# Two-layer graph and expert kernel: the first layer's second expert product in seven block products, its shares computed at the listing

## The chip, the cores and the metric

One core of one Trainium2 chip. The metric is the device time of one execution in microseconds, the median of several runs. Matrices are float32. Engines: PE (TensorE, matmuls), DVE (VectorE), ACT (ScalarE), POOL (GpSimd), SP (SyncE, which issues most loads).

## The reference

Two layers over 3327 nodes with 256 features, each an aggregation over a sparse matrix followed by a mixture of 8 experts of which each node uses 2. Cut to layer 0 (layer 1 has another aggregation, Gelu and experts with 256 hidden units):

```python
x = x + relu(adj @ (layernorm(x) @ W) + b)
t = layernorm(x)
gate_scores = einsum('bsd,ed->bse', t, Wg) + bg
topk_scores, topk_idx = top_k(gate_scores, 2)
topk_probs = softmax(topk_scores)
combine = sum(topk_probs[..., None] * one_hot(topk_idx, 8), -2)
for e in range(8):
    h = relu(einsum('bsd,hd->bsh', t, W1[e]) + b1[e])   # 1024 hidden
    y = einsum('bsh,dh->bsd', h, W2[e]) + b2[e]
    out = out + combine[..., e:e+1] * y
x = x + out
```

## The kernel before, in words

Nodes are padded to 3328 = 26 tiles of 128. `adj` comes in 13 panels of 256 rows, each in two pieces of 128 x 3328, in a ring of six places.

**Aggregation of layer 0** (`aggregate_first`). Panels 0 and 1 run side by side, panels 2 to 11 as five pairs with seven block products in place of eight (`pair`, sums of pieces on DVE), panel 12 alone (`rest`, whose matmuls are on L495). A finished panel waits; `finish` (called in `rest` after slice `first + BEHIND`, 5) or the next pair first lists what was routed before (`listed`), then multiplies the waiting sums by W (`weigh`, L506), and then routes them (`route0`). ACT meanwhile counts signs of `adj` (`count`, L1369, eight activations per piece, each with a read of its accumulator), which layer 1 needs.

**Routing.** `scores` multiplies each tile by each row of the gating matrix `gate` on DVE (L659), `weights` ranks the eight scores (`rt_both` marks the two best, L697) and computes the shares: the difference `rt_d` of the two scores on DVE (L724), its Exp on ACT (L725), and 1/(1+e) and its rest on DVE (L727 to L729). `list_tokens` later counts places by matmuls of `rt_both` (L760, L761), copies shares (L755) and ids into the rows on POOL, and scatters the rows to the experts' lists `xlist` (L779).

**Experts of layer 0** (`experts`, H = 1024). The lists are cut into 30 blocks: 26 pairs of 256 rows and 4 singles of 128, the first 8 pairs early, the rest by a table that `plan` computes on DVE from the counts. A block's rows, its expert's W1, b1, W2 and b2 (2.6 MB) take two places of the ring, so three blocks are in flight; SP issues block t+3 when block t has left its places. `step(t)` calls in this order:

- `first`: for each of 8 groups of 128 hidden units two matmuls (L1171) into `ps_h`, evacuated by ACT with Relu and b1 (L1178) into `hT`;
- `turned` for block t+1: four transposes (L1157) into `ptb`, which shares the two PSUM buffers of `ps_h`, copied by DVE (L1161, `copy`);
- `second`: for each half of 128 rows, eight matmuls of 256 columns (L1209) into `ps_y`, then b2 added (L1216) and the row's share multiplied (L1217) on DVE, and the rows scattered by POOL to `ys` (L779).

[...]The order is settled at build: mostly that of the calls, but a call may be put ahead of one that would have to wait, unless `behind` or `issue_after` hold it. `step(0)` has `finish_last` between its two products: the listing of panels 10 and 11, then the weighing and routing of panel 12. The listing of panel 12 follows `step(1)`. Around the last blocks DVE adds outputs that are complete (`add_begun`, behind block 27) and takes their statistics (behind block 28), for layer 1.

**After it**: `load_gate(gates[1])` loads the gating matrix of layer 1 over that of layer 0, by POOL's queue, as soon as panel 12 is listed. `between` normalizes and projects for layer 1, whose aggregation starts at 769 us.

Of the kernel before, what the change touches and what calls it, by code (L numbers as in the profile page):

```python
# [10 lines left out]
F32 = mybir.dt.float32  # L11
BF16 = mybir.dt.bfloat16
I32 = mybir.dt.int32
AF = mybir.ActivationFunctionType
ALU = mybir.AluOpType
# [7 lines left out]
P = 128  # L23
NT = 26
NP = NT * P
D = 256
DC = D // P
# [3 lines left out]
NPAN = NP // PW  # L31
NCHUNK = 2
CJ = NT // NCHUNK
# [41 lines left out]
    return order + [q for q in range(LATE_PAIRS, LATE) if q not in order]  # L75


BEHIND = 5
BEGUN, FIRST_TILES, MORE_TILES = 12, 14, 22
WARM = 54  # L80
TIERS = 3
# [46 lines left out]
def gnn_moe_two_layers(  # L128
# [353 lines left out]
    def aggregate_first(b_sb, w, w_sb, begin, count, route, listed, freed):  # L482
# [69 lines left out]
            else:  # L552
                freed(pan, k)

        def rest(pan, first, hooks=()):
            hooks = dict(hooks)
            for j in range(first, NT):
                add(pan, j)
                if j == first + BEHIND:
                    finish()  # L560
                if j in hooks:
                    hooks[j]()
            g = sums_of()
            for c in range(DC):
                copy(g[:, c, :], sums[pan][c])
            waiting.append((pan, g))
# [76 lines left out]
        sums[NPAN - 1] = banks[0:2]  # L643
        for _ in range(NCHUNK):
            count_next()
        rest(NPAN - 1, 0, {CJ: layer0.turn_first})
        return finish

    def rows_of(a, t0, n):
# [64 lines left out]
        nc.vector.tensor_reduce(v, m, AX.X, ALU.add)  # L714
        return v

    def weights(sc, n, bias=None):


        if bias is not None:  # L720
            nc.vector.tensor_tensor(sc, sc, bias.unsqueeze(1).to_broadcast([P, n, E]), ALU.add)
        sel, top, both = top_two(sc, n)
        d = work.tile([P, n], F32, name="rt_d", bufs=2)
        nc.vector.tensor_tensor(d, top[:, :, 1], top[:, :, 0], ALU.subtract)  # L724
        nc.scalar.activation(d, d, AF.Exp)  # L725
        w = work.tile([P, n, K], F32, name="rt_w", bufs=2)
        nc.vector.tensor_scalar(w[:, :, 0], d, 1.0, None, ALU.add)  # L727
        nc.vector.reciprocal(w[:, :, 0], w[:, :, 0])
        nc.vector.tensor_tensor(w[:, :, 1], w[:, :, 0], d, ALU.mult)  # L729
        return sel, both, w  # L730

    def normalized(t, n, on_scalar=False):

# [15 lines left out]

    def list_tokens(xns, sel, both, w, t0, n, xlist, group):  # L750

        for i, xn in enumerate(xns):
            at = 2 * i
            nc.gpsimd.tensor_copy(xn[:, :, 1, 0:D], xn[:, :, 0, 0:D])
            nc.gpsimd.tensor_copy(xn[:, :, :, WT], w[:, at : at + 2, :])  # L755
            nc.gpsimd.tensor_copy(xn[:, :, :, ID], ids[:, t0 + at : t0 + at + 2, :])
        pr = pst.tile([P, n, E], F32, name="pr", tag="pt")
        for g in range(n):
            i = t0 + g
            nc.tensor.matmul(pr[:, g, :], lhsT=before, rhs=both[:, g, :], start=True, stop=False)  # L760
            nc.tensor.matmul(pr[:, g, :], lhsT=ones_sq, rhs=cum[:, i, :], start=False, stop=True)  # L761
            nc.vector.tensor_tensor(cum[:, i + 1, :], cum[:, i, :], both[:, g, :], ALU.add)
        row = work.tile([P, n, E], F32, name="rt_row", bufs=2)
        nc.vector.tensor_tensor(
            row, pr, starts.unsqueeze(1).to_broadcast([P, n, E]), ALU.add
        )
        idx = work.tile([P, n * K], I32, name="rt_idx", bufs=2)
        nc.vector.tensor_copy(idx, chosen(sel, row, n).rearrange("p n k -> p (n k)"))
        for g in range(n):
            for k in range(K):  # L770
                q = g * K + k
                row_ = xns[g // 2][:, g % 2, k, :]
                d = scatter(xlist, idx[:, q : q + 1], row_, "rows" + group)
                tc.declare_no_dep(d.ins, group="early" + group, reason="not rows of full blocks")
                rows_written.append(d)
# [270 lines left out]
        nc.vector.tensor_tensor(aside, spare_, aside, ALU.subtract)  # L1046
        return end

    def experts(xlist, ys, group, fixed, n_hidden, func, w1T, b1, w2T, b2, copy, order_of_places, kept=None):

# [42 lines left out]
        def col_of(t):  # L1095
            return t if t < EARLY else order[t - EARLY]

        def groups_of(t):
            return SG if t < EARLY or order[t - EARLY] < LATE_PAIRS else 1
# [61 lines left out]
            copy(xT, pt)  # L1161
            return xT

        def first(xT, w1, bb1, n):

            hT = blk("narrow" if kept else "wide", hc_n * SB)
            hT = hT.rearrange("p (c b) -> p c b", b=SB)[:, :, 0 : n * P]
            for hc in range(hc_n):
                ps = psh.tile([P, n * P], F32, name="ps_h", tag="ph")
                for c in range(DC):  # L1170
                    nc.tensor.matmul(  # L1171
                        ps,
                        lhsT=w1[:, c, ts(hc, P)],
                        rhs=xT[:, c, :],
                        start=(c == 0),
                        stop=(c == DC - 1),
                    )
                nc.scalar.activation(hT[:, hc, :], ps, func, bias=bb1[:, hc : hc + 1])  # L1178
            return hT

        def second(t, late, hT):
            _, xb, _, _, w2, bb2 = loaded[t]
            col, n = col_of(t), groups_of(t)
            index = work.tile([P, SG], I32, name="index", bufs=6)[:, 0:n]
            with behind(last_y):
                if t < EARLY:
                    nc.vector.tensor_copy(index, xb[:, :, ID])
                else:
                    _, own, aside = late[0:3]
                    index_f = index.bitcast(F32)  # L1190
                    nc.vector.tensor_tensor(index_f, xb[:, :, ID], own[:, col, 0:n], ALU.mult)
                    nc.vector.tensor_tensor(index, index_f, aside[:, col, 0:n], ALU.add)
            if t >= own_n:
                e = expert(t, late, [PE, DVE])
                w2 = all_w2[:, ds(e, 1), :, :].rearrange("p o c d -> p (o c) d")
                bb2 = all_b2[:, ds(e, 1), :].rearrange("p o d -> p (o d)")
            if not kept:
                y = blk("narrow", SG * D).rearrange("p (g d) -> p g d", d=D)
            else:
                if not several:  # L1200
                    wide = blk("wide", H // P * SB)
                    for at in range(0, H // P * SB, SG * D):
                        y = wide[:, at : at + SG * D]
                        several.append(y.rearrange("p (g d) -> p g d", d=D))
                y = several.pop(0)
            for g in range(n):
                ps = psy.tile([P, D], F32, name="ps_y", tag="py")
                for hc in range(hc_n):
                    last_product[:] = [nc.tensor.matmul(  # L1209
                        ps,  # L1210
                        lhsT=hT[:, hc, ts(g, P)],
                        rhs=w2[:, hc, :],
                        start=(hc == 0),
                        stop=(hc == hc_n - 1),
                    )]
                nc.vector.tensor_tensor(y[:, g, :], ps, bb2, ALU.add)  # L1216
                last_y[:] = [nc.vector.tensor_scalar(  # L1217
                    y[:, g, :], y[:, g, :], xb[:, g, WT : WT + 1], None, ALU.mult
                )]
                d = scatter(ys, index[:, g : g + 1], y[:, g, :], "outputs" + group)  # L1220
                tc.declare_no_dep(d.ins, group="read" + group, reason="not rows read by then")
                outputs.append(d)

        ready = {}

# [5 lines left out]
        def step(late, end=always, place=None, between=None):  # L1231

            t = len(started)
            started.append(t)
            while len(loaded) < min(t + RING // places, end):
                load(late)
            if t not in ready:
                ready[t] = turned(loaded[t][1], groups_of(t))
            _, _, w1, bb1, _, _ = loaded[t]
            hT = first(ready.pop(t), w1, bb1, groups_of(t))  # L1240
            if between:
                between()
            if t + 1 < min(len(loaded), end):
                ready[t + 1] = turned(loaded[t + 1][1], groups_of(t + 1), place)
            second(t, late, hT)

        def steps_to(late, stop):
            while len(started) < stop:
# [116 lines left out]
    def count(pan, k, copied):  # L1365
# [7 lines left out]

    layer0 = experts(
        xlist0, ys0, "0", FIXED[0], H, AF.Relu, f0_w1T, f0_b1, f0_w2T, f0_b2,
        nc.vector.tensor_copy, BLOCKS0,
    )

    def tiles_of(pans):
# [36 lines left out]
        list_waiting()  # L1416


    load_gate(gates[1])
    by_feature(None, g1_wp, proj_sb)  # L1420
    nc.gpsimd.dma_start(out=gnn_b_sb, in_=g1_bg[0:1, :].partition_broadcast(P))
    ng = NPAN * PW // GROUP
# [86 lines left out]

    def between():  # L1510

        normal.clear()
        second.clear()
        waiting = []
# [42 lines left out]
    def after1(layer1, pan):  # L1557
# [1 line left out]
        list_waiting()  # L1559
        xns = normalized(t, n)  # L1560
        sc = scores(xns, n) if pan < NPAN - 1 else scores_by_product(by_features(xns[0], n), n, f1_r_sb)
        routed.append((xns, *weights(sc, n), t, n, xlist1, "1"))
        x_t = x[:, t : t + n, :]
        nc.gpsimd.tensor_tensor(x_t, x_t, xns[0][:, :, 0, 0:D], ALU.add)
        if pan == EARLY_PANS[1]:
# [278 lines left out]
```

## Time and profile before

| | |
|---|---|
| median of 3 runs | 1220.21 us (1218.53 to 1228.95) |
| profiled execution | 1222.4 us, span 1220.7 us |
| layer 0's aggregation | up to 302.3 us |
| layer 0's experts | 302.3 to 717.8 us |
| PE busy | 1176.8 us |
| DVE busy | 755.1 us |
| ACT busy | 524.4 us |
| POOL busy | 288.2 us |

The page sums up one execution. A group line names the source line, engine, operation, what it writes and reads, the shape and count, then busy time and the mean duration of one, then idle time of the engine ahead of it. The slices divide the span in 40 parts of 30.5 us and show the busy share in tenths. A timeline line has start, length, engine, line, operation, shape and count of a run of equal instructions, and in brackets how long the engine had been idle before it and what ended that. Every float32 matmul call shows as two instructions.

### The profile page before, as it was taken

The page shows a single profiled execution, that of the slowest core. Times are in us where ns is not written, and L with a number is a line of the kernel's source. Part 1 is how long each engine was busy: PE and PEld are TensorE (multiplying, and loading weights), DVE is VectorE, ACT ScalarE, POOL GpSimd, SP SyncE. Part 2 cuts the span into 40 slices and gives each one's busy share as a digit, 9 for nine tenths or more (in the row PEclk, how much of TensorE's full clock was granted, in tenths as well). Part 3 has the DMA queues.
Part 4 walks back from the last instruction along what each step waited for, and adds up shares of the span by engine and source line. Part 5 has one row for each costly group of instructions (what it writes and reads, how often), then busy time and mean ns, then how long its engine had stood idle before and what let it go on. Part 6 is the DMA issues. An engine that isn't in the chain of part 4 may idle for free. (4 is left out here: it accounts for less than half of the span.)

```text
span 1220.7 us, 18191 instructions
## 1 busy us (share of the span) xinstructions
PE 1176.8 (96%) x5689; PEld 1008.2 (83%) x5689; DVE 755.1 (62%) x2767; ACT 524.4 (43%) x977; POOL 288.2 (24%) x367
## 2 busy tenths in 40 slices
PE   8999999999899999999999999999999999988983
PEld 7888888888688888888888888888888888877863
DVE  7699999988761111111121359289999998784464
ACT  5689566521222222323222236985555542132331
POOL 1112233043421111111111110022242242264441
PEclk9999999999899999999999999999999999988996
DMA  9894747654376555756565946154455452556696
GB/s 344 187 317 189 246 160 202 226 178 139 99 243 209 185 191 172 263 177 219 195 213 181 366 160 230 56 186 180 143 196 186 149 185 66 175 176 213 207 294 214
DMA packets 123178, 241.59 MB, mean 198 GB/s; under 512 B 24480, under 2 KB 93120, under 8 KB 116160
## 3 DMA queue, kind: packets, MB, share of 16 engines
q1 hardware_dynamic: 108656, 205.59, 51.0%
q0 software_dynamic: 11136, 31.60, 7.0%
q10 hardware_dynamic: 3280, 3.15, 0.7%
q8 instruction: 47, 0.77, 0.3%
q14 instruction: 59, 0.48, 0.1%
HBM read 203.98 MB, written 36.33 MB: 197 GB/s over the span
## 5 line engine op out<-in xcount | busy, mean ns | idle before, releaser
L440 PE MATMUL ps_g<-s,ring 128*128 128x256 f32 x1352 | 294.2, 380 | 0.0
L440 PEld LDWEIGHTS ps_g<-s,ring 128*128 128x128 f32 x1352 | 256.3, 190 | 34.0
L1178 ACT ACTIVATE pad<-ps_h,ring 128x256 f32<-128x256 f32 (+1 forms) x282 | 128.3, 457 | 346.3 <-PE ps_h L1171 321.7
L1171 PE MATMUL ps_h<-pad,ring 128*128 128x256 f32 (+1 forms) x1184 | 259.0, 372 | 9.5 <-ACT pad L1178 6.0
L1171 PEld LDWEIGHTS ps_h<-pad,ring 128*128 128x128 f32 x1184 | 205.8, 193 | 55.0 <-ACT pad L1178 18.9
L1209 PE MATMUL ps_y<-ring,pad 128*128 128x256 f32 x928 | 209.7, 382 | 0.0
L659 DVE SCALAR_TENSOR_TENSOR rt_product<-xn,gate 128x256 f32<-128x256 f32 x400 | 195.1, 488 | 16.2 <-ACT xn L360 2.2
L779 POOL DMA_INDIRECT ys<-pad,index x114 | 112.9, 990 | 390.5 <-DVE pad L1217 259.4
L1209 PEld LDWEIGHTS ps_y<-ring,pad 128*128 128x128 f32 x928 | 173.9, 192 | 22.1 <-issue 0.2
L779 POOL DMA_INDIRECT xlist<-xn,rt_idx x104 | 114.5, 1101 | 154.4 <-DVE ln_nw L347 56.3
L1369 ACT ACTIVATE sign<-ring,below 128x416 bf16<-128x416 f32 x208 | 133.4, 642 | 11.6 <-DMA ring<-in_adjT 5.6
L470 PE MATMUL ps_g<-ring,pad 128*128 128x256 f32 x520 | 115.5, 380 | 0.7 <-DMA ring<-in_adjT 0.5
L1216 DVE TENSOR_TENSOR pad<-ps_y,ring 128x256 f32<-128x256 f32 x64 | 27.1, 423 | 136.2 <-PE ps_y L1209 127.8
L470 PEld LDWEIGHTS ps_g<-ring,pad 128*128 128x128 f32 x520 | 98.3, 190 | 14.8 <-DMA ring<-in_adjT 0.9
L1161 DVE COPY pad<-ptb 128x512 f32<-128x512 f32 (+1 forms) x29 | 18.9, 652 | 144.6 <-PE ptb L1157 143.6
L1534 ACT ACTIVATE ring<-ring 128x3328 f32<-128x3328 f32 x22 | 65.4, 2979 | 87.6 <-DVE ring L1533 50.2
L470 PE MATMUL ps_g<-ring,s 128*128 128x256 f32 x390 | 89.6, 379 | 0.1
L470 PEld LDWEIGHTS ps_g<-ring,s 128*128 128x128 f32 x390 | 74.1, 190 | 10.4 <-ACT xnT L538 0.5
L480 DVE TENSOR_TENSOR ring<-ring,ring 128x768 f32<-128x768 f32 (+1 forms) x80 | 79.8, 1013 | 0.0
L495 PE MATMUL ps_g<-ring,s 128*128 128x256 f32 x312 | 68.5, 380 | 3.0 <-ACT s L360 3.0
L495 PEld LDWEIGHTS ps_g<-ring,s 128*128 128x128 f32 x312 | 59.0, 190 | 11.6 <-ACT s L360 3.6
L1535 ACT ACTIVATE ring<-ring 128x3328 f32<-128x3328 f32 x22 | 65.4, 2977 | 0.6
(220 smaller groups left out, 1114.8 us busy)
## 6 DMA issues: line engine op xcount, KB each, us to landing
ring<-in_adjT SPq DMA_DIRECT2D x50, 1664.0 KB
ring<-in_f_w1T SPq DMA_DIRECT2D x30, 1024.0 KB
ring<-in_f_w2T SPq DMA_DIRECT2D x30, 1024.0 KB
ring<-xlist SPq DMA_DIRECT2D x52, 258.0 KB
ring<-in_f_w SPq DMA_DIRECT2D x36, 256.0 KB
ring<-ys SPq DMA_DIRECT2D x12, 512.0 KB
ring<-in_f_b SPq DMA_DIRECT2D x34, 128.0 KB
xlist<-h2T SPq DMA_DIRECT2D x16, 257.0 KB
```

The source lines that it names most:

```text
L440: nc.tensor.matmul(ps[it], lhsT=chunks[k][:, c, ts(it, P)], rhs=s[:, j, :], start=(j == 0), stop=(j == NT - 1),)
L470: nc.tensor.matmul(ps, lhsT=b[:, c, :], rhs=a[:, c, :], start=(first and c == 0), stop=(c == CJ - 1), skip_group_check=not first,)
L480: nc.vector.tensor_tensor(out[:, part, :], out[:, part, :], other[:, part, :], ALU.add)
L495: nc.tensor.matmul(sums[pan][c], lhsT=s[:, j, ts(c, P)], rhs=piece(pan, j // CJ)[:, j % CJ, :], start=(j == 0), stop=(j == NT - 1),)
L659: nc.vector.scalar_tensor_tensor(product, xn, 1.0, gate[:, e, :], ALU.mult, ALU.mult, accum_out=sc[:, g, e : e + 1],)
L779: d = nc.gpsimd.indirect_dma_start(out=a[:, :], out_offset=bass.IndirectOffsetOnAxis(ap=index, axis=0), in_=rows_, in_offset=None,)
L1171: nc.tensor.matmul(ps, lhsT=w1[:, c, ts(hc, P)], rhs=xT[:, c, :], start=(c == 0), stop=(c == DC - 1),)
L1178: nc.scalar.activation(hT[:, hc, :], ps, func, bias=bb1[:, hc : hc + 1])
L1209: last_product[:] = [nc.tensor.matmul(ps, lhsT=hT[:, hc, ts(g, P)], rhs=w2[:, hc, :], start=(hc == 0), stop=(hc == hc_n - 1),)]
L1369: nc.scalar.activation(sign, piece(pan, k)[:, :, ts(i, GROUP)], AF.Sign, bias=below, accum_out=positive[:, pan, i, k : k + 1],)
L1534: nc.scalar.activation(a, a, AF.Square)
L1535: nc.scalar.activation(a, a, AF.Tanh)
```

## The change

**Second product of layer 0, pairs from block 3 on.** With `hT` cut into A11, A12 (hidden halves, first 128 rows), A21, A22 (second 128 rows) and W2 into B11, B12, B21, B22 (hidden halves by feature halves), seven products of 128 rows, 512 hidden units and 128 columns take the place of eight. `prepare`, called ahead of `first`, makes four differences of W2 on DVE, which lie in `gate`, and scales b2 by each row's share into `y` on ACT. `difference` and the start of `second_seven` make four sums of `hT` on DVE, in tiles named xnT and h2T. Each finished product or sum of products is multiplied by the share and added to a quarter of `y` in one DVE instruction (eight per block). Two of the four PSUM tiles are used again while they hold a sum.

**Shares of layer 0.** `weights` leaves the difference; Exp, 1/(1+e) and the copy into the rows are called in `list_tokens`. Layer 1 keeps the old place (`now=True`).

**Others.** The listing in the last panel comes after slice 8 instead of 5. The turned rows of layer 0 are copied by ACT instead of DVE. `gate` is loaded for layer 1 at the start of `between`.

```diff
-BEHIND = 5
+BEHIND, LAST_BEHIND = 5, 8
...
-        rest(NPAN - 1, 0, {CJ: layer0.turn_first})
+        rest(NPAN - 1, 0, {CJ: layer0.turn_first}, LAST_BEHIND)
...
-        nc.scalar.activation(d, d, AF.Exp)
+        if now:
+            nc.scalar.activation(d, d, AF.Exp)
+            return sel, both, shares(d, n)
+        return sel, both, d
...
     def list_tokens(xns, sel, both, w, t0, n, xlist, group):
+        if group == "0":
+            nc.scalar.activation(w, w, AF.Exp)
         for i, xn in enumerate(xns):
             at = 2 * i
             nc.gpsimd.tensor_copy(xn[:, :, 1, 0:D], xn[:, :, 0, 0:D])
-            nc.gpsimd.tensor_copy(xn[:, :, :, WT], w[:, at : at + 2, :])
...
+        if group == "0":
+            w = shares(w, n)
+        for i, xn in enumerate(xns):
+            nc.gpsimd.tensor_copy(xn[:, :, :, WT], w[:, 2 * i : 2 * i + 2, :])
...
+        def prepare(t):
+            _, xb, _, _, w2, bb2 = loaded[t]
...
+            nc.vector.tensor_tensor(t1, halves(w2, 0, 1), halves(w2, 0, 0), ALU.subtract)
+            nc.vector.tensor_tensor(t2, b22, t1, ALU.subtract)
+            nc.vector.tensor_tensor(t4, b21, t2, ALU.subtract)
+            nc.vector.tensor_tensor(t3, b22, halves(w2, 0, 1), ALU.subtract)
+            y = blk("narrow", SG * D).rearrange("p (g d) -> p g d", d=D)
+            for g in range(SG):
+                nc.scalar.activation(y[:, g, :], bb2, AF.Copy, scale=xb[:, g, WT : WT + 1])
...
+        def difference(sums, hT):
+            a11, a21 = halves(hT, 0, 0), halves(hT, 0, 1)
+            nc.vector.tensor_tensor(sums[1][2], a11, a21, ALU.subtract)
...
                 nc.scalar.activation(hT[:, hc, :], ps, func, bias=bb1[:, hc : hc + 1])
+                if sums and hc == hc_n // 2 - 1:
+                    difference(sums, hT)
...
+        def second_seven(t, late, hT, sums):
...
+            nc.vector.tensor_tensor(s1, a21, a22, ALU.add)
+            nc.vector.tensor_tensor(s2, s1, a11, ALU.subtract)
+            nc.vector.tensor_tensor(s4, a12, s2, ALU.subtract)
+            ps_x, ps_q, ps_b, ps_z = (
+                psy.tile([P, P], F32, name="ps_y", tag="py") for _ in range(4)
+            )
+            def multiply(ps, a, b, first=True):
+                for c in range(hc_n // 2):
+                    last_product[:] = [nc.tensor.matmul(
+                        ps, lhsT=a[:, c, :], rhs=b[:, c, :], start=(first and c == 0),
+                        stop=(c == hc_n // 2 - 1), skip_group_check=not first,
+                    )]
+            def put_in(g, half_, ps):
+                part = y[:, g, ts(half_, P)]
+                last_y[:] = [nc.vector.scalar_tensor_tensor(
+                    part, ps, xb[:, g, WT : WT + 1], part, ALU.mult, ALU.add
+                )]
+            multiply(ps_x, a11, b11)
+            put_in(0, 0, ps_x)
+            multiply(ps_q, a22, t4)
+            put_in(1, 0, ps_q)
+            multiply(ps_b, a12, b21)
+            put_in(0, 0, ps_b)
+            multiply(ps_z, s1, t1)
+            put_in(1, 1, ps_z)
+            multiply(ps_x, s2, t2, False)
+            put_in(0, 1, ps_x)
+            multiply(ps_z, s4, b22, False)
+            put_in(0, 1, ps_z)
+            put(y, index, 0)
+            multiply(ps_x, s3, t3, False)
+            put_in(1, 0, ps_x)
+            put_in(1, 1, ps_x)
+            put(y, index, 1)
...
             _, _, w1, bb1, _, _ = loaded[t]
+            sums = prepare(t) if seven and t >= seven and groups_of(t) == SG else None
...
-        nc.vector.tensor_copy, BLOCKS0,
+        nc.scalar.copy, BLOCKS0, seven=3,
...
-    load_gate(gates[1])
...
     def between():
+        load_gate(gates[1])
```

## The prediction

> **What bounds the kernel now.** I read the page first: TensorE (PE) is busy 96% of the span and next to all of it in most slices, VectorE (DVE) is full only in the first quarter.
>
> ```profile
> PE 1176.8 (96%) x5689; PEld 1008.2 (83%) x5689; DVE 755.1 (62%) x2767; ACT 524.4 (43%) x977; POOL 288.2 (24%) x367
> ...
> PE   8999999999899999999999999999999999988983
> ...
> DVE  7699999988761111111121359289999998784464
> ```
>
> The change lies in the experts of layer 0, so next the timeline of PE there, 400 to 440 us: a block of 256 rows is first product, four transposes, second product, with no gap.
>
> ```profile
> 400.56 7.16 PE L1171 MATMUL ps_h<-pad,ring 128*128 128x256 f32 x32
> 407.55 0.60 PE L1157 MATMUL ptb<-ident,ring 128*128 128x128 f32 x4
> 407.98 7.07 PE L1209 MATMUL ps_y<-ring,pad 128*128 128x256 f32 x32
> 414.89 7.16 PE L1171 MATMUL ps_h<-pad,ring 128*128 128x256 f32 x32
> ```
>
> The starts give a block of 14.33 us: 6.99, 0.43 and 6.91. One matmul of the code is two instructions here (16 calls, x32), so an instruction of 256 columns takes 6.91 / 32 = 216 ns; the mean of 382 ns in the groups is a pipelined duration, not a price. From 400 to 690 us the windows view has PE busy 289.72 of 290 us, DVE 51.45 and ACT 79.89. So PE alone sets the time of this stage, and each ns taken from its stream counts.
>
> The new products have 128 columns. The group of that shape reads 24.8 us for 176 instructions, 141 ns each, but that takes in waits and pipeline ends. The timeline of PE at 554 us, in a single block (128 rows), is closer:
>
> ```profile
> 554.13 1.05 PE L1171 MATMUL ps_h<-pad,ring 128*128 128x128 f32 x8
> 555.02 0.60 PE L1209 MATMUL ps_y<-ring,pad 128*128 128x256 f32 x2
> 555.46 1.05 PE L1171 MATMUL ps_h<-pad,ring 128*128 128x128 f32 x8
> ```
>
> Eight take 555.02 - 554.13 = 0.89 us, 111.5 ns each, a new weight load in front of every one. (L1209 also stands here between matmuls that the code calls earlier: at build, a call may be put ahead of one that would wait.)
>
> Last the seam between aggregation and experts, 271 to 320 us, PE and then ACT:
>
> ```profile
> 271.92 5.34 PE L495 MATMUL ps_g<-ring,s 128*128 128x256 f32 x24
> 278.58 0.18 PE L760 MATMUL pr<-rt_both,before 128*128 128x8 bf16 x1 [1.32 <-DVE rt_both L697]
> ...
> 302.28 5.34 PE L1171 MATMUL ps_h<-pad,ring 128*128 128x256 f32 x24
> 311.63 3.78 PE L1171 MATMUL ps_h<-pad,ring 128*128 128x256 f32 x8 [4.01 <-ACT pad L1178]
> ...
> 315.46 2.94 PE L506 MATMUL ps_o<-proj_sb,xnT 128*128 128x256 f32 x8
> ```
>
> ```profile
> 305.93 0.47 ACT L1178 ACTIVATE pad<-ps_h,ring 128x256 f32<-128x256 f32 x1 [0.39 <-PE ps_h L1171]
> 311.01 0.21 ACT L725 ACTIVATE rt_d<-rt_d 128x4 f32<-128x4 f32 x1 [4.61 <-DVE rt_d L724]
> ```
>
> PE waits 1.32 us for the routing of a panel pair, then 4.01 us for ACT: in ACT's queue the Exp of L725 stands ahead of the evacuations of block 0, and it waits 4.61 us for DVE. After both waits PE runs slow: the windows view grants a clock of 0.78 from 277 to 284.6 us and 0.81 from 302.3 to 320.
>
> [...]
>
> **The change, part by part.**
>
> *Seven products.* Removed per pair: 16 calls, 32 instructions x 216 = 6.91 us. Added: 7 products x 4 calls x 2 = 56 instructions x 111.5 = 6.24 us. Gain 0.66 us. Of the 30 blocks of layer 0, 26 are pairs and 4 singles; from block 3 on, 23 pairs. 23 x 0.66 = **15.2 us**. The longest run of this shape in the trace is 8, so 56 in a row is bounded: 109 ns (the transposes, 0.43 us for 4) gives 18.5 us, 115 gives 10.8. I take 111.5.
>
> *DVE's new work.* Per block 8 sums and differences of 128x512 elements, at 0.69 us (L1293, 128x512, 689 ns[...]): 5.5 us. 8 evacuations of 128x128 from PSUM: the 128x256 one (L1216) takes 423 ns[...], between 200 and 423: 2.3 us. Index 0.3. Together 8.1 us (7.4 to 9.2) in a block of 13.67; 2.5 us of evacuation, copy and scaling go. Order: from the end of the first product, PE has transposes and three products, 0.43 + 3 x 0.89 = 3.1 us, until it needs s1. That is ready after the last ACT evacuation (0.65) and one sum, 1.4 us; s2 is ready at 2.1 and needed at 4.0, s4 at 2.8 and 4.9. The differences of w2 (2.8 us) run under the first product of the same block. So PE does not wait: cost 0. Without that cover the whole chain of 2.1 us would stand in front of the products.
>
> *ACT* gets the turned copy (0.59 us, L1161 on ACT) and two scalings of b2 (some 0.45 each) on top of 8 x 0.47: 5.3 us of 13.67. The copy has 6.2 us until the next block. The scalings stand ahead of block t's evacuations and need b2 of t and the scatter of block t-2 done, both over 10 us old. Cost 0. Loads: SP issues block t+3 when block t ends, as before; 2.6 MB take some 9 us of 13.67 (issued at 372.9, the DMA share falls at 382).
>
> *Exp at the listing.* The Exp is no longer ahead of block 0's evacuations: the 4.01 us wait goes. *Listing 3 slices later:* 3 x 4 x 216 = 2.6 us more work ahead of the listing's matmuls, more than 1.32: that wait goes, with the 1.8 us that the slow clock cost behind it (16 matmuls from 279.31 to 284.57, 5.26 us for 3.45). So the last panel ends at 302.28 - 3.1 = 299.2, block 0's first product at 306.1. Now the listing's matmuls need rt_both: DVE had it at 310.1, and sheds there the copy L1161 with the wait and slow scores around it, some 2.3 us: 307.8. The wait moves to PE itself, 1.7 us. Then the two panel products, 1.73 us: 309.8 where they ended at 318.23. Gain 8.4 us; if the wait costs a slow window again (8 x 0.21), 6.7. I take **7.5 us**. Behind the waiting matmuls stand the two products that feed DVE with the last panel; its routing took 19.5 us from there and PE now comes to its listing 21 us later, so nothing is late next. A further 1.98 us gap at 329 us I leave as it is. The three DVE operations of the shares move along. In the paired panels they could wait for ACT behind eight Sign counts (8 x 0.83 = 6.6 us), but DVE has 8 us of piece sums in that place: 0.
>
> *What gets a new wait.* Between the last blocks DVE adds the begun outputs (690.5 to 697.5 us) and takes their statistics (704.8 to 712.3), called ahead of the next block's differences. If DVE keeps the order of calls, the differences end 2.8 us after that: in block 28 the second product waits for t4 until 699.9 where PE is there at 697.8, then 0.3 for s1, 2.4 us; in block 29 likewise 2.8 us. **+5.2 us**, 0 if the differences are put ahead; I take 4. Queued behind are only these blocks' own evacuations.
>
> *Gate load later.* POOL issues it after the last scatters, some 721 us. [...]it meets the load of the next outputs (issued 722.0, needed 738 with 3 us to spare): 0 to 2, I take 0.5. The scores that need it come after 790.
>
> Sum: -15.2 - 7.5 + 4 + 0.5 = -18.2 us. The profiled execution took 1222.4 us (span 1220.7, 1.7 around it), 2.2 above the median of 1220.21; moved to the median, **1202 us**.
>
> **The rivals.**
>
> *Given back by new waits.* DVE waits for ACT's Exp at each listing of the paired panels, where it is busy 75.5 of 80 us (180 to 260) and PE 80 of 80, and the seam gains nothing: -15.2 + 5.2 + 0.5 = -9.5, 1211 us; with three such waits of 2 us, 1217. For it: DVE's high share there. Against: the cover above. 0.19.
>
> *Weight loads become the bound, and it ends slower.* A load reads 190 ns in every group, and 83% of PEld's time is taken with 256 columns to hide it. If a long run of 128 columns takes 141 ns, as the group's row says, 56 of them take 7.9 us, +1.0 per block, +22.7, and with the other terms -3.0: 1240 us. It turns slower than before from 111.5 + (18.2 us / 23 / 56 = 14) = 126 ns. Against: at 554 us loads follow each other at 111 ns. 0.08.
>
> *DVE too slow for the chain of sums.* It would take 13.67 / 8.1 = 1.7 times my prices to bound the block; at twice, 16.2 us, +1.9 per block, 1254 us. [...]0.03.
>
> *The products do what they should and the seam does too, with the end stalls gone:* 1198; part of the likeliest case.
>
> **How the numbers follow.** Likeliest, 0.70: its parts' ends give 1222.4 - 18.5 - 8.4 - 2 = 1193.5 and 1222.4 - 10.8 - 6.7 + 7.2 = 1212, less 2.2: 1191 to 1210. With given back (1207 to 1219) the range reaches 1216 and leaves out the two slow rivals and the edges. A measurement of this kernel can tell about 1% from no change: 12.2 us, 1208 us. Faster by more: nearly all of the likeliest, 0.69; within 1%: 0.19; slower by over 1%: the slow rivals and mishaps not seen, 0.12.
>
> **What would show it.** Right: second products of 56 instructions in 6.2 to 6.3 us, blocks at 13.7 us with PE full from 345 to 680; no wait of ACT for rt_d at 306, a wait of PE for rt_both below 2 us in its place; DVE near 60% and ACT near 40% in the experts. Wrong: a spacing above 120 ns within a product, waits of PE for DVE's sums in every block, gaps in the paired panels between 90 and 270 us.

## The result, and the profile after

The changed kernel takes 1324.24 us, the median of 4 runs (1322.34 to 1326.88), beside 1221.73 us of the kernel before (4 runs): a ratio of 1.0818 (95% interval 1.0787 to 1.0849). Predicted were 1202 us, 1191 to 1216. The profiled execution has a span of 1325.2 us, 104.5 us more than the one of before.

The page, in the lines that were shown of before:

```profile
PE 1206.6 (91%) x6241; PEld 1040.7 (79%) x6241; DVE 868.2 (66%) x3013; ACT 556.1 (42%) x1053; POOL 291.0 (22%) x367
...
PE   9999999998988788778787889999999999998993
...
DVE  7799999888543344234243448748999999865454
...
PEclk9999999999987899878889899999999999999997
```

From slice 11 to 23 (counted from 0), the experts of layer 0, PE was full and is now busy for 7 to 8 tenths, and its clock, at 9 in every one of these slices before, reads 7 to 9. Everything after that stage takes as long as before: block 29 starts at 810.0 us for 703.9, and from there to the end it is 515.2 us for 516.8.

The timeline of PE in one block, to be set against the block of 14.33 us that the prediction shows:

```profile
411.59 3.65 PE L1214 MATMUL ps_h<-pad,ring 128*128 128x256 f32 x16
417.07 1.13 PE L1214 MATMUL ps_h<-pad,ring 128*128 128x256 f32 x4 [1.84 <-ACT pad L1221]
420.49 5.28 PE L1214 MATMUL ps_h<-pad,ring 128*128 128x256 f32 x12 [2.28 <-ACT pad L1221]
425.61 0.60 PE L1169 MATMUL ptb<-ident,ring 128*128 128x128 f32 x4
426.04 1.06 PE L1260 MATMUL ps_y<-ring,pad 128*128 128x128 f32 x8
...
432.30 1.89 PE L1214 MATMUL ps_h<-pad,ring 128*128 128x256 f32 x8
```

The block takes 20.71 us. Its seven products (L1260) take 432.30 - 426.04 = 6.26 us, without a wait. The loss is in the first product (L1214), which the change does not touch: it takes 14.02 us where it took 6.99. It stops after 16 and after 20 of its 32 instructions, each time for ACT, which has to evacuate `ps_h` (L1221). The last 12 take 425.61 - 420.49 = 5.12 us, 427 ns each in place of 216. By starts, 2.0 and 2.6 us are waits and 2.5 us slow clock, together some 7.0 us, what the block has too many.

Why ACT is late, in its own timeline in the same stretch:

```profile
413.58 0.47 ACT L1221 ACTIVATE pad<-ps_h,ring 128x256 f32<-128x256 f32 x1 [0.40 <-PE ps_h L1214]
416.15 0.51 ACT L1193 ACTIVATE pad<-ring,ring 128x256 f32<-128x256 f32 x1 [2.10 <-DMA ys<-pad,index]
416.56 0.46 ACT L1221 ACTIVATE pad<-ps_h,ring 128x256 f32<-128x256 f32 x1
419.57 0.51 ACT L1193 ACTIVATE pad<-ring,ring 128x256 f32<-128x256 f32 x1 [2.55 <-DMA ys<-pad,index]
419.98 0.82 ACT L1221 ACTIVATE pad<-ps_h,ring 128x256 f32<-128x256 f32 x2
```

and when POOL issued the scatters of `ys`:

```profile
412.00 0.97 POOL L790 DMA_INDIRECT ys<-pad,index  x1 [18.35 <-DVE gate L1189]
413.27 0.97 POOL L790 DMA_INDIRECT ys<-pad,index  x1 [0.30 <-ACT pad L1221]
```

L1193 is the scaling of b2 in `prepare`. It stands in ACT's queue behind the second and the third evacuation of a first product and waits there for a scatter. The scatters waited for were issued at 412.00 and 413.27, as the block before ended, and let ACT go 4.2 and 6.3 us later. The evacuations behind are ready, since PE's first 16 instructions had ended by 415.24 us, but none passes: they run at 416.56 and 419.98, right behind the scalings. Whose scalings these are, the line's own record tells (count, shortest, median and longest in ns, first and last start):

```profile
L1193 ACT ACTIVATE pad<-ring,ring x46: 495/507/508, 338.4 to 803.1; 128x256 f32<-128x256 f32 x46
```

The 46 are two for each of the 23 blocks with seven products, from block 3 to block 29. The first runs at 338.4 us, in the first product of block 2, which begins at 336.20; block 3 begins only at 352.74. The last runs at 803.1 us, in block 28; block 29 begins at 809.95. So the scaling of block t+1 was put ahead into the first product of block t. `y` has two places that take turns, so `y` of block t+1 lies where that of block t-1 lies, and the scatter of block t-1 has just been issued.

How much it comes to, in the group's row and in the waits from 360 to 780 us (total, times, longest):

```profile
L1193 ACT ACTIVATE pad<-ring,ring 128x256 f32<-128x256 f32 x46 | 23.2, 506 | 103.5 <-DMA ys<-pad,index 97.6
```

```profile
ACT pad L1193 <- DMA ys<-pad,index: 79.9, 34, 4.9
PE ps_h L1214 <- ACT pad L1221: 66.2, 30, 4.6
```

The scaling itself costs 23.2 us of ACT in the whole kernel; what it waits for costs 103.5.

Windows over the same block show when the clock goes (PE busy, then PEld, DVE, ACT, POOL; then the granted clock, DMA share, GB/s):

```profile
411.60:415.20 3.60, 3.60 (x18) 2.68 (x16) 1.48 (x5) 0.95 (x2) 1.94 (x2) 1.00 0.42 97
415.20:418.60 3.40, 1.17 (x5) 0.68 (x4) 0.00 (x0) 0.87 (x2) 0.00 (x0) 1.00 1.03 401
418.60:422.00 3.40, 1.51 (x4) 1.24 (x5) 0.69 (x1) 1.23 (x3) 0.00 (x0) 0.50 0.93 310
422.00:425.60 3.60, 3.60 (x10) 2.78 (x9) 0.00 (x0) 0.95 (x2) 0.00 (x0) 0.52 0.00 0
```

After a stretch in which PE is busy for 1.17 of 3.40 us, the clock is halved (0.50), from about 418.6 us to 425.4. From 360 to 680 us its mean is 0.87, where the kernel before has 1.00.

The fuller the DMA engines were, the longer these three scatters held their scalings: one issued at 335.67 us, with a DMA share of 0.14 until it let go, 2.7 us; that of 412.00, with 0.60, 4.2 us; that of 413.27, with 0.96, 6.3 us. SP issues the 2.6 MB of block t+3 in the same moment as the scatters of block t-1, and from 415.2 to 422 us the DMA share is 1.03 and 0.93. That this load is the reason fits, but no run has these scatters without it.

Not every block has such waits. Of the 23 blocks with seven products 17 take 16.3 to 21.2 us; the other six take 13.3 to 13.7 us, at a clock of 1.00. Four of the six stand ahead of a single block, which has no scaling to put ahead; in block 25 the scalings of block 26 stand behind its last evacuation and the copy; and block 29 is the last. Block 25, PE and then ACT:

```profile
753.04 7.16 PE L1214 MATMUL ps_h<-pad,ring 128*128 128x256 f32 x32
...
766.72 7.16 PE L1214 MATMUL ps_h<-s,ring 128*128 128x256 f32 x32
```

```profile
761.46 0.91 ACT L1193 ACTIVATE pad<-ring,ring 128x256 f32<-128x256 f32 x2 [0.20 <-issue]
```

These six run the same 56 instructions of 128 columns and the same sums on DVE without a wait. The four single blocks, into which the scalings of the next pair are put, take 11.7 to 14.4 us for 7.8 before.

The seam went as the prediction had it: no wait at 278 us for the routing, none of block 0's evacuations for Exp, and a wait of PE for `rt_both` in their place, then the gap in block 1:

```profile
307.59 0.17 PE L767 MATMUL pr<-rt_both,before 128*128 128x8 bf16 x1 [1.98 <-DVE rt_both L697]
...
322.96 5.45 PE L1214 MATMUL ps_h<-pad,ring 128*128 128x256 f32 x24 [1.91 <-ACT pad L1221]
```

### The profile page after: what moved, and what is told of

The parts are those of the page before. It is cut to its first block, busy times and chain, and to the rows that moved or that the text cites. A ratio compares the mean times of both kernels' runs of the same rounds, so it can differ in the third digit from the quotient of the medians.

```text
span 1325.2 us, 19711 instructions
## 1 busy us (share of the span) xinstructions
PE 1206.6 (91%) x6241; PEld 1040.7 (79%) x6241; DVE 868.2 (66%) x3013; ACT 556.1 (42%) x1053; POOL 291.0 (22%) x367
## 5 line engine op out<-in xcount | busy, mean ns | idle before, releaser
L1214 PE MATMUL ps_h<-pad,ring 128*128 128x256 f32 (+1 forms) x1184 | 300.6, 409 | 74.2 <-ACT pad L1221 70.1
L1214 PEld LDWEIGHTS ps_h<-pad,ring 128*128 128x128 f32 x1184 | 230.0, 213 | 132.3 <-ACT pad L1221 88.7
L1221 ACT ACTIVATE pad<-ps_h,ring 128x256 f32<-128x256 f32 (+1 forms) x282 | 125.4, 454 | 316.6 <-PE ps_h L1214 253.2
L1205 DVE TENSOR_TENSOR h2T<-pad 128x512 f32<-128x512 f32 x23 | 15.9, 691 | 123.9 <-ACT pad L1221 123.9
L1251 DVE TENSOR_TENSOR xnT<-pad 128x512 f32<-128x512 f32 x23 | 15.9, 692 | 94.2 <-ACT pad L1221 94.2
L1267 DVE SCALAR_TENSOR_TENSOR pad<-ps_y,ring,pad 128x128 f32<-128x128 f32 x184 | 62.0, 348 | 15.7 <-PE ps_y L1260 15.4
L1193 ACT ACTIVATE pad<-ring,ring 128x256 f32<-128x256 f32 x46 | 23.2, 506 | 103.5 <-DMA ys<-pad,index 97.6
```

Source lines behind the costliest of these rows:

```text
L1214: nc.tensor.matmul(ps, lhsT=w1[:, c, ts(hc, P)], rhs=xT[:, c, :], start=(c == 0), stop=(c == DC - 1),)
L1267: last_y[:] = [nc.vector.scalar_tensor_tensor(part, ps, xb[:, g, WT : WT + 1], part, ALU.mult, ALU.add)]
```

## The experiments

Twelve runs in three sets (9 is the kernel before itself, 10 that of experiment 1 again); each set has its own runs of the kernel before on its chip, and the chips differ: the kernel before takes 1222.5, 1206.6 and 1223.5 us. Ratios are to these, and times are compared within a set only. The changed kernel was not run again in them; the kernel before took 1221.7 us beside it, 0.8 us from that of the first set. Three theories: **A**, the scaling of b2, put ahead in ACT's queue, waits for a scatter just issued; **B**, the long stream of 128 columns brings down the clock or is bound by its weight loads; **C**, other new work (DVE's sums, the copy on ACT, the moved shares) makes the waits.

**1. The scalings held behind the block's own evacuations** (`last_hidden` is the last evacuation of its first product).

```diff
-            for g in range(SG):
-                nc.scalar.activation(y[:, g, :], bb2, AF.Copy, scale=xb[:, g, WT : WT + 1])
...
             hT = first(ready.pop(t), w1, bb1, groups_of(t), sums)
+            if sums:
+                with tc.issue_after(last_hidden[0].ins):
+                    for g in range(SG):
+                        nc.scalar.activation(
+                            sums[2][:, g, :], loaded[t][5], AF.Copy,
+                            scale=loaded[t][1][:, g, WT : WT + 1],
+                        )
```

> The changed kernel whole, but the two scalings of b2 are issued on ACT behind the last evacuation of the same block's first product, so none of them is put ahead into another block. Theory A (in ACT's queue a scaling put ahead waits for a scatter of the block before that was just issued, the evacuations behind it wait too, PE stops twice per block and loses its clock): the two waits per block go, a block takes 13.7 to 14.0 us instead of 20.7, the granted clock in the experts is 1.0, 1198 to 1212 us. Theory B (the long stream of 128 columns itself brings the clock down, or its weight loads set the pace): the clock stays near 0.87 and the time above 1270 us. Theory C (DVE's sums are late): PE waits for DVE remain at the second products, above 1250 us.

Measured: 1206.6 us, ratio 0.9865 (0.9835 to 0.9896). A block on PE, in the timeline:

```profile
395.58 7.16 PE L1212 MATMUL ps_h<-pad,ring 128*128 128x256 f32 x32
402.58 0.60 PE L1169 MATMUL ptb<-ident,ring 128*128 128x128 f32 x4
403.01 1.06 PE L1260 MATMUL ps_y<-ring,pad 128*128 128x128 f32 x8
...
409.27 2.13 PE L1212 MATMUL ps_h<-pad,ring 128*128 128x256 f32 x9
```

and the row of the held scaling (its line is L1343 here):

```profile
L1343 ACT ACTIVATE pad<-ring,ring 128x256 f32<-128x256 f32 x46 | 20.6, 496 | 0.0
```

One block takes 409.27 - 395.58 = 13.69 us, with no gap, and from 360 to 680 us the clock is 1.00. The same 46 scalings wait 0.0 us. Theory A holds, and B is out: all 56 instructions of 128 columns are still there. So is C for these waits, but for one place, block 28 (experiment 7).

**2. The scalings still put ahead, three places for `y`.**

```diff
-            y = blk("narrow", SG * D).rearrange("p (g d) -> p g d", d=D)
+            y = y_place().rearrange("p (g d) -> p g d", d=D)
```

`y_place` goes round the two narrow places and one more that the later arms of the kernel use for turned rows.

> The changed kernel whole, with the scalings of b2 put ahead as they are, but the outputs y of the pair blocks go round three places instead of two, so that a scaling waits for the scatter of one block earlier, some 14 us old. Theory A: the scalings no longer wait on ACT, blocks of 13.7 to 14.0 us at a clock of 1.0, 1198 to 1212 us, the same as with the scalings held to within 5 us. Theory B: above 1270 us, clock near 0.87. If it were the place of the scaling in the queue alone, without the wait for a scatter (0.5 us of ACT each in the wrong spot), this one stays above 1270 us where the held one is fast.

Measured: 1216.47 us, ratio 0.995 (0.9933 to 0.9966), 4 us over the upper end that A gave. From 373 to 680 us the blocks take 13.67 us at a clock of 1.00: it was the age of the scatter, and not the place in the queue. The 10 us to the first experiment are elsewhere, most of them in one place, ACT and then PE in block 3:

```profile
357.15 0.91 ACT L1202 ACTIVATE pad<-ring,ring 128x256 f32<-128x256 f32 x2 [11.13 <-DMA ring<-in_f_b]
```

```profile
358.47 7.70 PE L1223 MATMUL ps_h<-pad,ring 128*128 128x256 f32 x22 [4.82 <-ACT pad L1230]
```

These scalings (L1202) belong to block 4, stand ahead of the evacuations of block 3 and wait for the load of block 4's b2, which SP issued at 348.64 us, so the operand that the prediction took for old is young as well. With the slow clock behind it (0.95 in the mean from 330 to 400 us; the 22 instructions take 7.70 us, at 216 ns each they would take 4.75), block 3 takes 21.3 us where it should take 13.7. So an operation put ahead waited for whichever of its operands came last: for a load here (11.13 us), for a scatter in the changed kernel (2.10 and 2.55 us).

**3. All but the seven products.**

```diff
-        nc.scalar.copy, BLOCKS0, seven=3,
+        nc.scalar.copy, BLOCKS0,
```

> The changed kernel without the seven products: eight products in all blocks, and all the other parts (shares at the listing, last listing three slices later, copy of the turned rows on ACT, gate loaded later). Theory A: no scaling is put ahead, so nothing is lost in the experts: blocks of 14.3 us, and the seam's gain of 7.5 us with 0.5 for the gate, 1211 to 1216 us. Theory C (copy on ACT or the moved shares make the waits): above 1240 us.

Measured: 1218.16 us, ratio 0.996 (0.9944 to 0.9976). From block 3 on the clock is 1.00 and blocks take 14.3 us: copy, shares and gate load make no wait there. The seam brings 4.4 us here, less than the 7 expected; see experiments 5 to 11.

**4. Eight products, only the scalings added.** In place of adding b2 and multiplying, DVE multiplies the product by the share and adds the scaled b2; the scalings are called ahead of `first`, as in the changed kernel.

```diff
-            sums = prepare(t) if seven and t >= seven and groups_of(t) == SG else None
-            hT = first(ready.pop(t), w1, bb1, groups_of(t), sums)
+            y = scaled_b2(t) if seven and t >= seven and groups_of(t) == SG else None
+            hT = first(ready.pop(t), w1, bb1, groups_of(t))
...
+                    last_y[:] = [nc.vector.scalar_tensor_tensor(
+                        y[:, g, :], ps, xb[:, g, WT : WT + 1], y[:, g, :], ALU.mult, ALU.add
+                    )]
```

> Eight products of 256 columns as in the kernel before, with all other parts of the change; of the seven products' work only the two scalings of b2 on ACT are kept, called ahead of the first product as in the changed kernel with the outputs in two places, and one DVE operation per half adds the product to them. No sums or differences on DVE, no stream of 128 columns. Theory A: if the scalings are put ahead as in the changed kernel, they wait for a scatter just issued, and the kernel is slow without any product of 128 columns: 1290 to 1345 us, clock in the experts 0.86 to 0.9. Theory B and C: 1211 to 1220 us, clock 1.0.

Measured: 1333.78 us, ratio 1.0932 (1.0885 to 1.0978), as slow as the changed kernel with none of its products or sums, and 115.6 us over experiment 3, which has the same parts but for the scalings and the DVE operation that adds to them. The scaling's row (L1184 here):

```profile
L1184 ACT ACTIVATE pad<-ring,ring 128x256 f32<-128x256 f32 x46 | 23.2, 506 | 193.1 <-DMA ys<-pad,index 172.7
```

The scalings alone make the whole loss; their place in the queue is a little other (one goes in behind the third evacuation, one ahead of the first), and they wait 193 us. The clock from 360 to 690 us is 0.93, higher than A expected, so here more of the loss is waiting and less of it slow clock.

**5 to 8. The seam and block 28**, on the kernel of experiment 1, on the second chip. That kernel itself was not run on this chip, so the four are read against each other.

```diff
-BEHIND, LAST_BEHIND = 5, 8
+BEHIND, LAST_BEHIND = 5, 5
```

> The kernel with the held scalings, and the last panel pair's listing back at 5 slices in place of 8. If the later listing brought the 3.1 us by which the first expert block starts sooner, the wait of 1.3 us at 278 us and the slow clock behind it come back, and this kernel takes 3 us more than the held one measured beside the same kernel before (1209 to 1211 against 1206.6). If the seam's gain is lost again in block 1 whatever comes ahead, it takes the same, within 1 us.

Measured: 1203.58 us, ratio 0.9966 (0.9952 to 0.998). The wait for the routing is back (1.49 us at 279 us), a wait of 4.0 us at 343 us comes in, and block 3 starts at 360.1 us; in the other three kernels of this set it starts at 351.9, 352.2 and 353.3. It takes 5.4 to 5.8 us more than experiments 8 and 6, where 3 were expected.

Experiment 6 moves POOL's loads behind the early blocks:

```diff
-    by_feature(None, g1_wp, proj_sb)
-    nc.gpsimd.dma_start(out=gnn_b_sb, in_=g1_bg[0:1, :].partition_broadcast(P))
...
     written = list(outputs)
+    by_feature(None, g1_wp, proj_sb)
+    nc.gpsimd.dma_start(out=gnn_b_sb, in_=g1_bg[0:1, :].partition_broadcast(P))
     layer0.steps_to(late, layer0.always - 5)
```

> The kernel with the held scalings, and the two loads that POOL issues for the next layer behind the last panel's eight listing scatters (proj_sb, gnn_b_sb) issued some ten blocks later. In all kernels but one the first evacuation of block 1 starts within 0.2 us of the end of the second of these issues, 3 us after its product was issued on PE. If these issues hold it up, the gap of 3.05 us at 323.8 us and the slow clock behind it go, and 4 to 5 us with them: 1202 us. If not, the gap stays at 2 to 3 us and the time within 1 us of the held one.

Measured: 1197.75 us, ratio 0.9926 (0.9904 to 0.9948). The gap in block 1 is gone, but it is gone in all four kernels of this chip, so this says nothing of the loads. Experiment 12 decides it.

Experiment 7 puts the additions in three pieces:

```diff
         layer0.step(late)
+        with behind(last_y):
+            add_begun(0, 1)
         layer0.step(late)
         with behind(last_y):
-            add_begun()
+            add_begun(1, 2)
         layer0.step(late)
         with behind(last_y):
+            add_begun(2)
             statistics(0, BEGUN, begun_stats)
```

> The kernel with the held scalings, and the six additions of begun outputs to x (7 us of DVE in one piece ahead of the sums of block 28) put in three pieces behind blocks 26, 27 and 28. If the 2.7 us wait of PE at 685.5 us in block 28 and the slow clock behind it (4.6 us together) come from that piece, they go: 1202 to 1203.5 us. If the outputs aren't loaded by then, DVE waits for a DMA ahead of block 27's sums and a wait of 2 us or more stands there instead: 1206 or more.

Measured: 1195.03 us, ratio 0.9895 (0.9871 to 0.9918), 2.7 us under experiment 6, but the two intervals overlap. What the trace shows it to take away is this, in PE's and DVE's timelines of experiment 1:

```profile
685.54 3.10 PE L1260 MATMUL ps_y<-gate,xnT 128*128 128x128 f32 x16 [2.70 <-DVE xnT L1251]
```

```profile
677.32 5.76 DVE L1402 TENSOR_TENSOR x<-x,s 128x1024 f32<-128x1024 f32 x5
683.00 0.68 DVE L1203 TENSOR_TENSOR h2T<-pad 128x512 f32<-128x512 f32 x1
683.60 1.22 DVE L1402 TENSOR_TENSOR x<-x,s 128x1024 f32<-128x1024 f32 x1
```

The six additions stand in DVE's queue ahead of the sum s1 (L1251), which PE needs for its fourth product. Block 28 takes 18.3 us there; with the additions spread it takes 13.7.

Experiment 8 undoes `now`: Exp and shares are called in `weights` again.

```diff
-        routed.append((xns, *weights(sc, n, f0_bg_sb), t, n, xlist0, "0"))
+        routed.append((xns, *weights(sc, n, f0_bg_sb, now=True), t, n, xlist0, "0"))
```

> The kernel with the held scalings, and the Exp and the shares back at the routing, as before the change. If the Exp at the listing is what removed the 4.0 us wait of block 0's evacuations, that wait comes back at 308 us with the slow clock behind it: 4 to 6 us more than the held one, 1211 to 1213. If the time saved there is lost again in block 1 anyway (gap of 3.05 us in place of 1.98, slow clock), it takes only 0 to 2 us more.

Measured: 1198.14 us, ratio 0.9932 (0.9907 to 0.9958), the same as experiment 6. With the later listing, PE itself waits for `rt_both` (2.06 us at 308 us), and Exp follows that by half a microsecond: the evacuation behind it is late for nobody. So on this chip the listing's place makes the seam's gain, and the Exp's place adds nothing that was measured.

**9 to 12. The kernel before, the held one, the seven products alone and the best parts together, side by side.**

> The kernel before, unchanged, for a profile of it on the same chip as the three beside it: the chip of the last four runs took 1.3% less than the one before it for the same kernel, and the stages at the seam and at the end differ. Ratio 1.00. Block 3 is expected to start 3 us later than in the kernel with the held scalings if the seam gives back its gain on every chip, and 7 to 8 us later if that was the one chip.

> The kernel with the held scalings again, beside the others of this set. Ratio 0.985 to 0.988 to the kernel before; blocks of 13.67 us, block 28 of some 18 us with PE waiting 2.4 to 2.7 us for the first sum.

Experiment 11 is the held kernel with the edits of experiments 5 and 8, experiment 12 that with the edits of 6 and 7.

> The seven products with the held scalings, and both parts of the seam undone: the listing of the last panel pair at 5 slices, and the Exp and shares at the routing. What it takes less than the kernel before is what the seven products bring: 23 blocks of 0.66 us, less the wait in block 28 (4.6 us), 10 to 11 us, ratio 0.991. What the held one takes less than this is what the seam brings: 3 us if the seam gives most of its gain back, 7 to 8 us if not.

> The held scalings with the six additions of begun outputs in three pieces and POOL's two loads for the next layer ten blocks later: 4 to 5 us less than the held one beside it from the additions, and 0 to 1 us (a chip where block 1 doesn't wait) or 4 to 5 us (a chip where it does, if those loads are the cause) from the loads: ratio 0.978 to 0.984 to the kernel before.

| kernel | us | ratio to before | block 3 starts | layer 1 starts |
|---|---|---|---|---|
| 9, before | 1223.45 | 1.0 (0.9982 to 1.0018) | 355.8 | 767.6 |
| 10, held | 1204.40 | 0.9847 (0.9818 to 0.9876) | 353.6 | 755.5 |
| 11, seven products alone | 1211.62 | 0.9914 (0.9884 to 0.9944) | 358.5 | 759.9 |
| 12, held, additions spread, loads later | 1204.43 | 0.9849 (0.9821 to 0.9877) | 353.2 | 752.0 |

The seven products bring 10.5 us by the ratio of experiment 11 (6.9 to 14.2), 11.9 by the medians, and the seam what experiment 10 takes less than 11: 8.2 us by the ratios, 7.2 by the medians. The profiles show less of the seam. Block 3 starts 4.9 us earlier in experiment 10 than in 11, and only 2.2 us earlier than in the kernel before (3 expected if most of the gain is given back). For in experiment 11, with both edits of the seam undone, it starts 2.7 us later than in the kernel before: the gap in block 1 is 3.10 us for 1.89, and PE waits 0.81 us for an evacuation in block 2, where the kernel before has no wait. Experiment 3, without the seven products, has both waits too (3.05 and 0.76 us). What these two kernels share at this place, and the kernel before lacks, is the copy on ACT. It is a suspect and no more: no run takes it out alone, and the same held kernel has 3.05 us in experiment 1 and 2.12 in experiment 10. The profiled executions of experiments 9 and 10 are 11.7 us apart, the medians 19: 2.2 us up to block 3, 9.9 from there to layer 1, and nothing behind it.

The gap in block 1 is 2.07 us in experiment 12 and 2.12 in experiment 10: POOL's loads are not its cause. Experiment 12 starts layer 1 3.5 us before experiment 10 and doesn't end sooner by the median, where 4 to 5 us less were expected: in the profiles its last stage, the experts of layer 1, takes 158.4 us for 156.2. That stage takes 154.7 to 158.4 us in this set's profiles with no change to it, so whether the 3.5 us are given back there for a reason, or lost in its spread, stays open. The held kernel beats both the kernel before and the changed one; nothing tried beats it on its own chip beyond the interval.

## Why the prediction was wrong, by its own steps

**The step that failed** is the one on ACT: "The scalings stand ahead of block t's evacuations and need b2 of t and the scatter of block t-2 done, both over 10 us old. Cost 0." It took the place in the queue from the order of the calls. The prediction says itself that a call may be put ahead of one that would wait; it weighed this for DVE's differences and not for the scalings. Put ahead by most of a block, the scaling of block t+1 meets the scatter of block t-1, which is 0 us old when block t begins; in place of 0 it waits, and makes the evacuations behind it wait. The experiments show the price: 1324.24 us with it, 1206.6 without, each with its interval far from the other, some 118 us; in one set, experiment 4 beside 3, 115.6. Of the 117.7 us between the two spans, 70.8 are PE's idle time (1325.2 - 1206.6 = 118.6 us by the page, for 1207.5 - 1159.7 = 47.8), and the rest, 47 us, PE is busy longer with the same matmuls. The mean clock, 0.948 for 0.986, accounts for that by estimate: 1159.7 x 0.986 / 0.948 = 1206.2 us.

ACT's wait becomes PE's by the order of the queue: in both waits above, of 2.10 and 2.55 us, ready evacuations stand behind the scaling and none goes ahead of it. And a scatter just issued is not free to wait for: the trace has 4.2 and 6.3 us from issue to release, beside a load of 2.6 MB, and 2.7 us at a DMA share of 0.14.

**The rivals.** None of them was it. "Given back by new waits" had the right kind (a new wait) at the wrong engine and stage. "Weight loads become the bound" is refuted: 56 instructions in 6.26 us are 111.8 ns each, without a gap. "DVE too slow" is refuted but for block 28: one sum takes 691 ns (taken 690), one evacuation of 128x128 348 ns (the 2.3 us taken for eight, 290 each, was an estimate, within 200 to 423). Its time of 1254 us is a slip: with the prediction's other terms, 1220.2 + 23 x 1.9 - 3.0, it comes to 1261.

**The other terms of the sum**, read from the kernels without the wait:

- Seven products with the stalls at the end: -15.2 + 4 = -11.2 predicted; 1218.16 - 1206.6 = 11.6 us in the first set, 10.5 to 11.9 in the third. Right. A block takes 13.67 to 13.69 us, 13.67 predicted.
- The stalls themselves: 5.2 us predicted (2.4 in block 28, 2.8 in block 29), 4 taken. Block 28 has all of it, 18.27 us for 13.67: the wait is 2.70 us, for s1 and not for t4, and the 16 instructions behind it take 3.10 us, where at 111.8 ns each they would take 1.79. Block 29 has none. Size right, place half right.
- The seam: -7.5 predicted. Up to block 0's second product it is right: the two waits go, the new one is 1.98 to 2.13 us (1.7 predicted), and the transposes start at 310.84 us in experiment 3 for 318.23, 7.4 earlier. Then part is lost: "A further 1.98 us gap at 329 us I leave as it is" held in the changed kernel (1.91), but the gap is 3.05 us in experiments 1 and 3, with a clock of 0.76 to 0.81 from 322 to 330 us, and another of 0.8 to 1.1 us comes in at 346 us. In experiment 3 block 1 takes 19.88 us for 17.12 and block 2 15.81 for 14.84, so block 3 starts 3.6 us earlier and not 7.4. By the times the seam brings 4.4 us (experiment 3) and 7.2 to 8.2 (experiment 10 beside 11). The term was too large up to block 3: the two blocks that it left as they were gave half of it back.
- "the 4.01 us wait goes" for the moved Exp: the wait goes, but by experiment 8 the later listing alone suffices for that on the second chip.
- Copy on ACT, shares in the paired panels, gate load: 0, 0 and 0.5 predicted. From block 3 on experiment 3 has no wait of this kind; whether the copy has a part in the new waits of blocks 1 and 2 is not shown.

With the wait on ACT gone, the times agree with the sum: 1204.4 and 1206.6 us with ratios of 0.9847 and 0.9865, where -18.2 us on 1220.21 is 0.9851. The seven products bear that out; the seam bears it out in part only, and the profiles of experiments 9 and 10 show 11.7 us in all, so that the agreement to a few us is in part luck. The lower end of the range also takes off 2 us for which the prediction names no term.

**What stays open**: why block 1's first evacuation is 2 to 3 us late on two chips and not on the third. It is not POOL's loads; scatters of the listing run at the same time, and no run here separates them. The kernel before has a gap there too (1.89 and 1.98 us).

## What to carry to other kernels

When a change adds an instruction that writes a buffer in rotation, ask where the build will put it and not where it is called, and work out its wait for the earliest place it can take: with two places, put ahead by one block, it waits for the transfer that has just been issued (4.2 and 6.3 us from issue to release here). In a queue where nothing passes it, as in ACT's here, its own length (0.5 us) is no measure of its cost (waits of 2.10 and 2.55 us); what counts is the age of its youngest operand, and who is queued behind it. Hold such an instruction behind the work that others wait for, or give its buffer one place more.

## What the runs showed of the hardware

- Half the clock came behind waits of PE. In the block shown, a wait of 1.84 us, 0.9 us of work and the first 0.4 us of the next wait went ahead of it; PE was busy for 1.17 of 3.40 us there. In the kernel before, the clock is 0.51 from 279.8 to 283.2 us, behind the wait of 1.32 us, and 0.51 from 310.7 to 317.5, which begins within that of 4.01 us. Behind waits of 1.91 us (changed kernel, 322.96) and 1.98 us (kernel before, 329.45) it stays at 1.00. So the length of the last wait does not settle it, and what does is not shown. In the changed kernel from 360 to 680 us, in steps of 0.2 us, the clock is 1.00 or 0.50 but for the steps in which it changes; of the thirteen halved stretches that lie whole in it, ten last 6.8 us and three 3.4 us.
- A scatter of 128 rows of 1 KB took 2.7 us from issue to the release of its waiter with the DMA engines 0.14 busy, and 4.2 and 6.3 us with 0.60 and 0.96, while 2.6 MB of loads were under way; from 415.2 to 418.6 us they moved 401 GB/s.
- Three chips took 1222.5, 1206.6 and 1223.5 us for the same kernel before. In the profiled kernels it is 144 to 147 us from the end of layer 1's aggregation to the end of the kernel on the second one, and 154 to 158 on the other two; so a gain of under 1% can only be read beside runs of the same set.
